# Context attention of a two-layer perceiver: nineteen score tiles in a queue, small operations moved off VectorE, keys from 96-row tiles, the last group turned in two parts

## The chip, the core and the metric

The kernel runs on one core of one Trainium2 chip. The metric is the device time of one execution in microseconds (us), as the median of several runs. The core has a matrix engine (TensorE, PE, with its weight loads shown apart as PEld), a vector engine (VectorE, DVE), a scalar engine (ScalarE, ACT), a general engine (GpSimd, POOL) and an engine that here only issues transfers (SyncE, SP). Each runs its own instructions in order; semaphores tie them together.

## The reference, cut to what matters

The whole kernel computes two layers on x (4 x 256 tokens of 256 features) with a context of 4 x 4096 vectors of 192 features. The part that the change touches is the context attention of layer 1:

```
h   = layernorm(x)                         # 4 batches x 256 tokens
q   = h @ Wq                               # 4 heads of 32
k   = ctx @ Wk                             # 4096 keys of 192 -> 4 x 32
s   = q @ k.T / sqrt(32) + mask            # per head 256 x 4096
w   = softmax over the 32 largest of each row, 0 elsewhere
c_t = mean over the 4 heads of w, @ ctx    # 256 x 192
```

The values are the context vectors themselves. c_t then steers a modulation of x, and a recurrence, a feed-forward block, self attention and a second feed-forward block follow.

## The kernel before

Layer 0 ends at about 1600 us. Then comes `l1_context` (L1073) in which 32 units of work are done: batch b (4), half of the tokens tt (2), head h (4), with 128 tokens each. Four units (the heads of one half) are a group. What one unit does:

- `scores(u)` (L1162 mask, L1165 scores, L1174 copy): 128 x 4096 scores in two steps. Each has four matmuls that add the mask and four of 32 rows that add q.k, into two PSUM tiles of 128 x 1024 from a pool of two; ACT copies each to an `sc` tile (eight of them: two units).
- `best` (L1186): 32 Max8 of DVE take the 8 largest of each 128 scores, 256 candidates in all.
- `chosen` (L1194 to L1203): four rounds of Max8 on the candidates, with a MatchReplace8 between the rounds, give the 32 largest in order (`top`). After the first round DVE makes `neg`, minus the largest (L1197). ACT computes exp(score + neg) into four tiles e of 128 x 1024 (L1201) and exp(top + neg) into `e32` (L1203).
- `weighted` (L1210 to L1216): DVE multiplies each e tile with (score >= the 32nd largest); it sums e32 (L1212), takes the reciprocal (L1213) and multiplies it by 0.25 and by a keep flag of the token (L1214). POOL multiplies the identity by that number into `diag` (L1216).
- `gathered` (L1229 to L1251) works per group, in four chunks of 1024 context positions. For each chunk 64 matmuls turn the weights: each e block of 128 x 128 is multiplied by its head's diag, and the four heads add up in PSUM (`ps_w`). Two ACT copies (L1237, `wT`) and then 16 matmuls with N = 193 (L1243) add the chunk to `ps_c`; the context tile's last column is 1, so that the weights' sum comes out too, which a later check reads. At the end ACT copies `ps_c` (L1249) and DVE takes the check (L1251).

The order is written by hand in the loop at the end of `l1_context`, and a scheduler then orders each engine's instructions by it. In the loop unit u is chosen and weighted, while unit u+1 has its Max8 and unit u+2 its scores. A group's gathering (`late`) begins at the end of its own last unit and goes on beside the next group's units: in each of them the context matmuls of one chunk, then the turning of the next one. `weights(u)` gives unit u of a group the four e tiles that hold chunk u of the preceding group, one of each head: so its exps wait for that chunk to be turned.

Beside it the keys of the next batch are computed in eight steps: `keys(b)` in `l1_context_keys` (L1032), one step in most of the units 0 to 5 of a batch, two in units 1 and 3. A step is two fp32 matmuls of 512 columns each over 128 and 64 of the 192 features (L1059, L1060) into the single PSUM tile "mm", an ACT copy to `ks` (L1062, two buffers) and four transfers that lay the heads' rows of ks into `kt` (L1064), which the scores read. The context comes in transposed, 768 KB for two steps, into two buffers (`context_keys`, L243). The single tile "mm" also serves the token transposes in unit 3 of a batch (`tokens`, L1117) and the queries in unit 6 (`queries`, L1130). `load_ctx` (L1146) loads a batch's context for the gathering into four tiles, each after a POOL memset of its last column; it is called in unit 3 of the next batch, when the gathering of the batch before is through. The keys of batch 0 are emitted ahead of the layer-0 feed-forward block and run beside its start, from 1490 us.

After the stage a flag is computed from the check and read from memory by all engines (`l1_context_again`, which holds a general version of the stage under an If); nothing of the next stage starts before that.

Of the kernel before, what the change touches and what calls it, by code (L numbers as in the profile page):

```python
# [11 lines left out]
F32 = mybir.dt.float32  # L12
# [219 lines left out]
def mask_rows(c, pool, mu):  # L232
# [10 lines left out]
def context_keys(c, pool, b, c4, queue=None):  # L243


    t = pool.tile([P, 1536], F32, tag="ctxT", name="ctxT")
    (queue or c.nc.sync).dma_start(t, c.a["ctxT"][b, c4])
    return t


def load_kk(c, pool, name, queue=None):
# [780 lines left out]
def l1_context_keys(c, es):  # L1032

    nc, tc = c.nc, c.tc
    w = Ctx()
    one = es.enter_context(tc.tile_pool(name="x1_kt", bufs=1))
    two = es.enter_context(tc.tile_pool(name="x1_ks", bufs=2))
    w.psum = es.enter_context(tc.tile_pool(name="x1_ps", bufs=1, space=PSUM))
    w.wk = load_kk(c, one, "x1_wku")
    w.wq = load_k(c, one, "x1_wq4")  # L1040
    w.keep = load(c, one, "x1_keep", [P, NB], dt=U8)
    w.kts = [one.tile([P, 4, G // 4], F32, tag=f"kt{i}", name=f"kt{i}") for i in range(2)]

    w.mask = one.tile([P, G // 4], BF16, tag="mask", name="mask")
    nc.vector.memset(w.mask, 0.0)
    w.pick = one.tile([P, B, P], BF16, tag="pick", name="pick")
    for b in range(B):
        nc.sync.dma_start(w.mask[b:P:32, :], c.mrowb[b].rearrange("(j k) -> j k", j=4))
        nc.vector.tensor_copy(w.pick[:, b, :], c.cols[:, 5 + b : 6 + b].to_broadcast([P, P]))

    def keys(b):

        kt = w.kts[b % 2]
        for c4 in range(4):
            ctxT = context_keys(c, two, b, c4)
            for j in range(2):
                hs = slice(64 * j, 64 * j + 64)
                ps = w.psum.tile([P, 512], F32, tag="mm", name="ps_k")
                nc.tensor.matmul(ps, w.wk[:, 0, :], ctxT[:, j * 512 : (j + 1) * 512], start=True, stop=False)  # L1059
                nc.tensor.matmul(ps, w.wk[hs, 1, :], ctxT[hs, 1024:1536], start=False, stop=True)  # L1060
                ks = two.tile([P, 512], F32, tag="ks", name="ks")
                nc.scalar.copy(ks, ps)  # L1062
                for h in range(4):
                    nc.sync.dma_start(  # L1064
                        kt[32 * c4 : 32 * c4 + 32, h, j * 512 : (j + 1) * 512], ks[32 * h : 32 * h + 32, :]
                    )
                yield

    w.keys = keys
    return w  # L1070


def l1_context(c, w, beside):  # L1073
# [13 lines left out]
    with ExitStack() as es:  # L1087
# [9 lines left out]

        keep = one.tile([P, NB], F32, tag="keep", name="keep")
        nc.vector.tensor_copy(keep, w.keep)
        off = one.tile([P, NB], F32, tag="off", name="off")  # L1100

        tiles = [ews.tile([P, 2, 512], F32, tag=f"e{i}", name=f"e{i}") for i in range(16)]

        def weights(u):
            h, odd = u % 4, u // 4 % 2
            return [tiles[4 * c4 + h if odd else 4 * h + c4] for c4 in range(4)]

        def tokens(b):

# [78 lines left out]
        def chosen(u):  # L1188

            top = two.tile([P, 32], F32, tag="top", name="top")  # L1190
            flat = cands.pop(u).rearrange("p n k -> p (n k)")
            for r in range(4):
                t8 = top[:, 8 * r : 8 * r + 8]
                nc.vector.max(t8, flat)  # L1194
                if r == 0:
                    neg = two.tile([P, 1], F32, tag="neg", name="neg")
                    nc.vector.tensor_scalar(neg, top[:, 0:1], -1.0, None, ALU.mult)  # L1197
                if r < 3:
                    nc.vector.match_replace(flat, t8, flat, TAKEN)
            for t, src in zip(weights(u), sc[u]):  # L1200
                nc.scalar.activation(t, src, AF.Exp, bias=neg)  # L1201
            e32 = two.tile([P, 32], F32, tag="e32", name="e32")
            nc.scalar.activation(e32, top, AF.Exp, bias=neg)  # L1203
            return top, e32

        def weighted(u, top, e32):

            b, tt, h = units[u]
            for t, src in zip(weights(u), sc.pop(u)):
                nc.vector.scalar_tensor_tensor(t, src, top[:, 31:32], t, ALU.is_ge, ALU.mult)  # L1210
            r = two.tile([P, 1], F32, tag="r", name="r")
            nc.vector.tensor_reduce(r, e32, AX.X, ALU.add)  # L1212
            nc.vector.reciprocal(r, r)  # L1213
            nc.vector.tensor_scalar(r, r, 0.25, keep[:, 2 * b + tt : 2 * b + tt + 1], ALU.mult, ALU.mult)  # L1214
            diag = two.tile([P, P], F32, tag=f"diag{h}", name=f"diag{h}")
            nc.gpsimd.tensor_scalar(diag, c.ident, r, None, ALU.mult)  # L1216
            return weights(u), diag

        def gathered(b, tt, es):

            ps_c = acc.tile([P, 512], F32, tag="acc", name="ps_c")
            n = 0
            for c4 in range(4):
                wTs = []
                for half in range(2):
                    ps = pst.tile([P, 512], F32, tag="pt", name="ps_w")
                    for i in range(4):
                        for h, (e, diag) in enumerate(es):
                            nc.tensor.matmul(  # L1229
                                ps[:, i * P : (i + 1) * P],  # L1230
                                e[c4][:, half, i * P : (i + 1) * P],
                                diag,
                                start=(h == 0),
                                stop=(h == 3),
                            )
                    wT = two.tile([P, 512], F32, tag="wT", name="wT")
                    nc.scalar.copy(wT, ps)  # L1237
                    wTs.append(wT)
                yield
                for half, wT in enumerate(wTs):  # L1240
                    for i in range(4):
                        t, j = c4 % 2 * 2 + half, c4 // 2 * 4 + i
                        nc.tensor.matmul(  # L1243
                            ps_c[:, : DC + 1], wT[:, i * P : (i + 1) * P], cxs[b][t][:, j, :], start=(n == 0), stop=(n == 31)
                        )
                        n += 1
                yield
            o = two.tile([P, DC], F32, tag="o", name="o")
            nc.scalar.copy(o, ps_c[:, :DC])  # L1249
            i = 2 * b + tt  # L1250
            nc.vector.tensor_tensor(off[:, i : i + 1], ps_c[:, DC : DC + 1], keep[:, i : i + 1], ALU.subtract)  # L1251
            nc.sync.dma_start(c.cn[:, i, :], o)
# [793 lines left out]
def _arrays(i):  # L2046
# [11 lines left out]
    for m in range(P):  # L2058
# [13 lines left out]
    ctxT = i["ctx_768"].transpose(0, 2, 1).reshape(B, DC, 4, 2, 512)  # L2072
    ctxT = np.concatenate(
        [ctxT[:, 0:P].transpose(0, 2, 1, 3, 4).reshape(B, 4, P, 1024), ctxT[:, P:].transpose(0, 2, 3, 1, 4).reshape(B, 4, P, 512)], 3
    )
    return {
        "x": i["x"],
        "ctx": i["ctx_768"],
        "ctxT": ctxT,
        "ctx6": i["ctx_768"].reshape(B, 4, 4, 256, 6, 32).transpose(0, 1, 2, 5, 4, 3).reshape(B, 4, P, 6, 256),  # L2080
        "gmask": i["mask_BxS2_bf1"].view(np.uint8),
        "cols": cols,
# [78 lines left out]
```

## Time and profile before

| | us |
|---|---|
| median of three runs (lowest, highest) | 2597.29 (2596.54, 2598.22) |
| profiled execution, its own time | 2590.52 |
| its span, first to last instruction | 2588.7 |
| mean granted TensorE clock | 0.93 |
| PE, DVE, ACT, POOL busy | 2395.8, 1658.9, 1064.9, 145.3 |
| the L1 context stage | about 1600 to 2180 |
| in it, one batch of 8 units (units 8 to 16, 16 to 24) | 143.3, 143.4 |

The profile is of one execution on the slowest core. Its busy shares are means over all stages, so a stage is read by asking the trace for its own window. A wait is listed as "engine, operation, line <- the engine, operation and line that released it". Matmul ends are modelled, so that a busy PE isn't PE at its peak. An operation's mean hides what lies beside it: the POOL operation of L1216 has a mean of 1417 ns in this stage, and single ones take from 604 to 2683 ns.

### The profile page before, as it was taken

What the parts mean: (1) busy time and instruction counts of PE and PEld (TensorE: products, weight loads), DVE (VectorE), ACT (ScalarE), POOL (GpSimd) and SP (SyncE); (2) the same over time, 40 slices, a digit from 0 to 9 for tenths busy, and PEclk for the clock granted to TensorE, in tenths of its full rate; (3) what the DMA queues carried; (4) which work ended last, traced back from release to release, by engine and by line L of the source; (5) the groups of instructions that cost most, each with busy time, mean ns of one, the idle gap of its engine ahead of it and who ended that gap; (6) DMA issues with size and microseconds to landing.
All of it is one profiled execution on the core that took longest, in us unless ns stands there. A gap on an engine that the chain in (4) does not pass through costs nothing. (4 is left out here: it accounts for less than half of the span.)

```text
span 2588.7 us, 54603 instructions
## 1 busy us (share of the span) xinstructions
PE 2395.8 (93%) x22673; PEld 1476.0 (57%) x22673; DVE 1658.9 (64%) x4043; ACT 1064.9 (41%) x1861; POOL 145.3 (6%) x176
## 2 busy tenths in 40 slices
PE   6999999999999999999899899989899988984896
PEld 4655555555555555555555544467676777453554
DVE  6666666666666666678644414988788892725544
ACT  1355554555455554556122112655555651010221
POOL 3000000000000000000000000010011010512000
PEclk7999999999999999999899989799999998996876
DMA  8321213121222213100100021203112004000110
GB/s 208 91 59 56 67 48 78 44 76 48 67 56 60 67 48 78 31 8 2 38 5 1 31 86 57 62 27 92 46 51 59 27 27 144 13 0 17 34 25 9
DMA packets 63374, 132.28 MB, mean 51 GB/s; under 512 B 11744, under 2 KB 38560, under 8 KB 62672
## 3 DMA queue, kind: packets, MB, share of 16 engines
q1 hardware_dynamic: 61616, 124.65, 17.1%
q8 instruction: 181, 2.97, 0.5%
q10 hardware_dynamic: 992, 3.02, 0.4%
q0 software_dynamic: 512, 1.05, 0.2%
q14 instruction: 73, 0.60, 0.1%
HBM read 98.17 MB, written 5.34 MB: 40 GB/s over the span
## 5 line engine op out<-in xcount | busy, mean ns | idle before, releaser
L512 DVE TENSOR_REDUCE mx<-ps_a 128x1 f32<-128x512 f32 x1024 | 659.3, 685 | 222.6 <-PE ps_a L497 218.9
L508 ACT ACTIVATE e<-ps_s 128x512 f32<-128x512 f32 x1024 | 555.7, 595 | 418.1 <-PE ps_a L497 397.8
L497 PE MATMUL ps_a<-kt,qa 32*128 32x512 f32 x2048 | 659.7, 649 | 10.9 <-DVE mx L512 7.7
L483 PE MATMUL ps_s<-qb,kt 32*128 32x256 f32 x4096 | 593.1, 402 | 0.0
L483 PEld LDWEIGHTS ps_s<-qb,kt 32*128 32x128 f32 x4096 | 350.6, 184 | 197.3 <-issue 106.4
L425 PE MATMUL o_ps<-e,v 128*32 128x256 f32 x4096 | 327.6, 391 | 0.0
L1229 PEld LDWEIGHTS ps_w<-diag,e 128*128 128x128 f32 x2048 | 242.8, 200 | 24.0 <-issue 21.7
L497 PEld LDWEIGHTS ps_a<-kt,qa 32*128 32x128 f32 x2048 | 231.8, 185 | 38.8 <-DVE mx L512 17.3
L1229 PE MATMUL ps_w<-diag,e 128*128 128x128 f32 x2048 | 248.5, 284 | 1.5 <-POOL diag L1216 1.5
L425 PEld LDWEIGHTS o_ps<-e,v 128*32 128x32 f32 x4096 | 81.0, 108 | 246.5 <-issue 235.0
L1186 DVE MAX8 cand<-sc 128x8 f32<-128x128 f32 x1024 | 212.1, 275 | 12.5 <-ACT sc L1174 12.4
L1210 DVE SCALAR_TENSOR_TENSOR e<-sc,top,e 128x1024 f32<-128x1024 f32 x128 | 159.2, 1278 | 32.7 <-ACT e L1201 32.7
L1201 ACT ACTIVATE e<-sc,neg 128x1024 f32<-128x1024 f32 x128 | 143.1, 1147 | 34.0 <-PE ps_w L1229 32.4
L1174 ACT COPY sc<-ps_s 128x1024 f32<-128x1024 f32 x128 | 126.4, 1007 | 48.0 <-PE ps_s L1165 46.3
L329 PE MATMUL ps_k<-ctxT,x_wk 32*128 32x256 f32 x1536 | 104.2, 400 | 12.4 <-DMA ctxT<-in_ctx 12.4
L351 PEld LDWEIGHTS ps_v<-x_wv,ctxT 32*128 32x128 f32 x3072 | 97.4, 190 | 15.4 <-DVE mx L512 9.4
L351 PE MATMUL ps_v<-x_wv,ctxT 32*128 32x128 f32 x3072 | 104.6, 279 | 0.7
L1243 PEld LDWEIGHTS ps_c<-cx,wT 128*128 128x128 f32 x512 | 88.6, 200 | 27.8 <-ACT wT L1237 10.6
L329 PEld LDWEIGHTS ps_k<-ctxT,x_wk 32*128 32x128 f32 x1536 | 89.1, 195 | 26.8 <-issue 18.1
L1243 PE MATMUL ps_c<-cx,wT 128*128 128x193 f32 x512 | 100.4, 349 | 2.0 <-ACT wT L1237 2.0
L824 POOL TENSOR_TENSOR x<-x,f_bo 128x256 f32<-128x256 f32 x8 | 5.8, 725 | 1538.0 <-DVE x L823 1510.8
L1165 PE MATMUL ps_s<-kt,q 32*128 32x512 f32 x512 | 87.8, 658 | 0.0
(401 smaller groups left out, 2548.3 us busy)
## 6 DMA issues: line engine op xcount, KB each, us to landing
ctxT<-in_ctx SPq DMA_DIRECT2D x62, 768.0 KB
kt<-ks SPq DMA_DIRECT2D x352, 64.0 KB
ctxT<-in_ctxT SPq DMA_DIRECT2D x16, 768.0 KB
cx<-in_ctx SPq DMA_DIRECT2D x16, 768.0 KB
x_w<-in_x_w SPq DMA_DIRECT2D x2, 1024.0 KB
qk<-rot SPq DMA_DIRECT2D x8, 256.0 KB
a_qk<-qk SPq DMA_DIRECT2D x16, 128.0 KB
ctxT<-in_ctx ACTq DMA_DIRECT2D x2, 768.0 KB
```

The lines of the kernel that those rows point to most:

```text
L329: nc.tensor.matmul(ps[:, :256], w.wk[hs, gp, k, :], ctxT[hs, k, :], start=(k == 0), stop=(k == 5))
L351: nc.tensor.matmul(ps[:, ks], ctxT[hs, k, ks], w.wv[hs, gp, k, :], start=(k == 0), stop=(k == 5))
L425: nc.tensor.matmul(o_pss[u][32 * h : 32 * h + 32, :S], vs[g // 2][:, c0 : c0 + 32], ew[h][:, n % 2, :], start=(n == 0), stop=(n == GT - 1),)
L483: nc.tensor.matmul(ps[:, k * S : (k + 1) * S], kts[u % 4 // 2][hs, u % 2, ks], qbs[u][hs, :], start=True, stop=True,)
L497: nc.tensor.matmul(ps, qas[u][hs, tt * P : (tt + 1) * P], kts[u % 4 // 2][hs, u % 2, ch * 512 : (ch + 1) * 512], start=True, stop=True,)
L508: nc.scalar.activation(e, ps.rearrange("p (k n) -> p k n", k=2), AF.Exp)
L512: nc.vector.tensor_reduce(mxs[u][:, tt, h, ch : ch + 1], ps, AX.X, ALU.max)
L1186: nc.vector.max(cands[u][:, n, :], sc[u][c4][:, i // 4, (i % 4) * P : (i % 4 + 1) * P])
L1201: nc.scalar.activation(t, src, AF.Exp, bias=neg)
L1210: nc.vector.scalar_tensor_tensor(t, src, top[:, 31:32], t, ALU.is_ge, ALU.mult)
L1229: nc.tensor.matmul(ps[:, i * P : (i + 1) * P], e[c4][:, half, i * P : (i + 1) * P], diag, start=(h == 0), stop=(h == 3),)
L1243: nc.tensor.matmul(ps_c[:, : DC + 1], wT[:, i * P : (i + 1) * P], cxs[b][t][:, j, :], start=(n == 0), stop=(n == 31))
```

## The change

There are four edits, all in the L1 context stage and its keys.

1. Nineteen e tiles in place of sixteen, given out in a queue that is computed ahead (`places`): a unit takes the four tiles at the queue's head, and the tiles of a chunk of the preceding group are put at its end. The first three tiles of a unit are thus spares, or were freed a chunk earlier; the fourth comes from the chunk just turned.
2. `neg` is computed by POOL; e32's sum is an output of ACT's exp (`accum_out`); the factor 0.25 and the keep flag are one table `quarter`, multiplied in by POOL's diag instruction. DVE keeps the reciprocal.
3. Keys from two tiles of 96 features: the context comes in another layout (`ctx96`), 384 KB for each step, and both the context tile and `ks` have one buffer.
4. The last group is gathered in two parts, heads 0 and 1, then heads 2 and 3, both into the same `ps_c`; the gathering of the group before it is pulled ahead in the units 29 and 30, and the first part's first two chunks are emitted in unit 30. The context matmuls of the last group are done for each part.

```diff
-    two = es.enter_context(tc.tile_pool(name="x1_ks", bufs=2))
-    w.wk = load_kk(c, one, "x1_wku")
+    w.wk = one.tile([96, 2, P], F32, tag="x1_wku", name="x1_wku")
+    nc.sync.dma_start(w.wk, c.a["x1_wku"].rearrange("(k p) n -> p k n", p=96))
...
         for c4 in range(4):
-            ctxT = context_keys(c, two, b, c4)
             for j in range(2):
-                hs = slice(64 * j, 64 * j + 64)
+                ctx = one.tile([96, 2, 512], F32, tag="ctx", name="ctx")
+                nc.sync.dma_start(ctx, c.a["ctx96"][b, 2 * c4 + j])
                 ps = w.psum.tile([P, 512], F32, tag="mm", name="ps_k")
-                nc.tensor.matmul(ps, w.wk[:, 0, :], ctxT[:, j * 512 : (j + 1) * 512], start=True, stop=False)
-                nc.tensor.matmul(ps, w.wk[hs, 1, :], ctxT[hs, 1024:1536], start=False, stop=True)
-                ks = two.tile([P, 512], F32, tag="ks", name="ks")
+                for k in range(2):
+                    nc.tensor.matmul(ps, w.wk[:, k, :], ctx[:, k, :], start=(k == 0), stop=(k == 1))
+                ks = one.tile([P, 512], F32, tag="ks", name="ks")
...
+        quarter = one.tile([P, NB], F32, tag="quarter", name="quarter")
+        nc.vector.tensor_scalar(quarter, keep, 0.25, None, ALU.mult)
...
-        tiles = [ews.tile([P, 2, 512], F32, tag=f"e{i}", name=f"e{i}") for i in range(16)]
+        tiles = [ews.tile([P, 2, 512], F32, tag=f"e{i}", name=f"e{i}") for i in range(19)]
+        places, free = [], list(tiles)
+        for u in range(len(units)):
+            if u > 3:
+                g, c4 = u // 4 - 1, u % 4
+                free += [places[4 * g + h][c4] for h in range(4)]
+            places.append(free[:4])
+            del free[:4]
         def weights(u):
-            h, odd = u % 4, u // 4 % 2
-            return [tiles[4 * c4 + h if odd else 4 * h + c4] for c4 in range(4)]
+            return places[u]
...
-                    nc.vector.tensor_scalar(neg, top[:, 0:1], -1.0, None, ALU.mult)
+                    nc.gpsimd.tensor_scalar(neg, top[:, 0:1], -1.0, None, ALU.mult)
...
-            nc.scalar.activation(e32, top, AF.Exp, bias=neg)
-            return top, e32
+            r = two.tile([P, 1], F32, tag="r", name="r")
+            nc.scalar.activation(e32, top, AF.Exp, bias=neg, accum_out=r)
+            return top, r
...
-            r = two.tile([P, 1], F32, tag="r", name="r")
-            nc.vector.tensor_reduce(r, e32, AX.X, ALU.add)
             nc.vector.reciprocal(r, r)
-            nc.vector.tensor_scalar(r, r, 0.25, keep[:, 2 * b + tt : 2 * b + tt + 1], ALU.mult, ALU.mult)
...
-            nc.gpsimd.tensor_scalar(diag, c.ident, r, None, ALU.mult)
+            i = 2 * b + tt
+            nc.gpsimd.tensor_scalar(diag, c.ident, r, quarter[:, i : i + 1], ALU.mult, ALU.mult)
...
-        def gathered(b, tt, es):
-            ps_c = acc.tile([P, 512], F32, tag="acc", name="ps_c")
+        def gathered(b, tt, es, ps_c, first, last):
...
-                                stop=(h == 3),
+                                stop=(h == len(es) - 1),
...
+            if not last:
+                return
...
             next(late, None)
+            if u == n - 3 or u == n - 2:
+                for _ in range(2):
+                    next(late, None)
+            if u == n - 2:
+                for _ in late:
+                    pass
+                ps_c = acc.tile([P, 512], F32, tag="acc", name="ps_c")
+                late = gathered(b, tt, group[:2], ps_c, True, False)
+                for _ in range(4):
+                    next(late, None)
...
-                late = gathered(b, tt, group)
+                if u == n - 1:
+                    late = gathered(b, tt, group[2:], ps_c, False, True)
+                else:
+                    late = gathered(b, tt, group, acc.tile([P, 512], F32, tag="acc", name="ps_c"), True, True)
```

More of the change, by code (lines that the diff above doesn't have):

```diff
@@ L240, in mask_rows @@
     nc.sync.dma_start(c.mrowb.rearrange("b (a k) -> (b a) k", k=S), mb)
[L243 to L248, printed above, removed]
 def load_kk(c, pool, name, queue=None):
@@ L1202, in chosen, with weighted @@
             e32 = two.tile([P, 32], F32, tag="e32", name="e32")
-            nc.scalar.activation(e32, top, AF.Exp, bias=neg)
-            return top, e32
-        def weighted(u, top, e32):
+            r = two.tile([P, 1], F32, tag="r", name="r")
+            nc.scalar.activation(e32, top, AF.Exp, bias=neg, accum_out=r)
+            return top, r
+        def weighted(u, top, r):
             b, tt, h = units[u]
@@ L1243, in gathered @@
                         nc.tensor.matmul(
-                            ps_c[:, : DC + 1], wT[:, i * P : (i + 1) * P], cxs[b][t][:, j, :], start=(n == 0), stop=(n == 31)
+                            ps_c[:, : DC + 1],
+                            wT[:, i * P : (i + 1) * P],
+                            cxs[b][t][:, j, :],
+                            start=(first and n == 0),
+                            stop=(last and n == 31),
                         )
@@ L2071, in _arrays @@
     causal[:, 1] = causal[:, 0].T
[L2072 to L2075, printed above, removed]
     return {
@@ L2078, in _arrays @@
         "ctx": i["ctx_768"],
-        "ctxT": ctxT,
+        "ctx96": i["ctx_768"].transpose(0, 2, 1).reshape(B, 2, 96, 8, 512).transpose(0, 3, 2, 1, 4),
         "ctx6": i["ctx_768"].reshape(B, 4, 4, 256, 6, 32).transpose(0, 1, 2, 5, 4, 3).reshape(B, 4, P, 6, 256),
```

## The prediction

> **What bounds the kernel now.** I read the page first: PE is busy 93% of the span and VectorE (DVE) 64%, but that average mixes stages. In the 40 slices of the page DVE stands at 7 to 9 tenths for eight slices on end, 26 to 33, and these are the stage that the diff touches (1600 to 2180 us). So I asked for the groups, the waits and short windows of that stage alone.
>
> The groups (line, engine, operation, shapes, count | busy us, mean ns of one | idle before it, releaser):
>
> ```profile
> L1229 PE MATMUL ps_w<-diag,e 128*128 128x128 f32 x2048 | 248.5, 284 | 1.5 <-POOL diag L1216 1.5
> L1186 DVE MAX8 cand<-sc 128x8 f32<-128x128 f32 x1024 | 212.1, 275 | 12.5 <-ACT sc L1174 12.4
> L1210 DVE SCALAR_TENSOR_TENSOR e<-sc,top,e 128x1024 f32<-128x1024 f32 x128 | 159.2, 1278 | 32.7 <-ACT e L1201 32.7
> L1243 PE MATMUL ps_c<-cx,wT 128*128 128x193 f32 x512 | 100.4, 349 | 2.0 <-ACT wT L1237 2.0
> L1194 DVE MAX8 top<-cand 128x8 f32<-128x256 f32 x128 | 54.0, 422 | 2.8
> L1199 DVE MATCH_REPLACE8 cand<-top,cand 128x256 f32<-128x256 f32 x96 | 39.2, 408 | 0.0
> L1214 DVE TENSOR_SCALAR r<-r,keep 128x1 f32<-128x1 f32 x32 | 6.7, 210 | 0.9
> L1212 DVE TENSOR_REDUCE r<-e 128x1 f32<-128x32 f32 x32 | 5.6, 174 | 3.7 <-ACT e L1203 3.7
> ```
>
> The reader sees two engines of nearly equal load. In the trace Max8 instructions start 0.195 us apart and the weighting 1.21 us apart, so one unit costs DVE 32 x 0.195 + 4 x 1.21 + 3.1 for the four rounds of the top 32 + 0.4 for the small operations = 14.6 us. PE needs 7.2 (64 turning matmuls) + 2.6 (16 context matmuls) + 2.4 (mask and scores) = 12.2, plus 2.1 for each key step: 14.3 with one key step, 16.4 with two. The shortest iterations of the stage are 14.57 us, by the starts of the turning chunks. With two key steps an iteration takes 22.2 us (1765.5 to 1787.8), with two steps and the token transposes 22.7, with queries and a key step 23.7. So each batch of 8 units loses most in three or four irregular iterations. The waits (us in total, times, longest) and the double step itself:
>
> ```profile
> DVE e L1210 <- ACT e L1201: 32.7, 26, 3.6
> ACT e L1201 <- PE ps_w L1229: 32.4, 19, 2.3
> PE ps_s L1162 <- ACT sc L1174: 24.0, 18, 1.6
> PEld ps_k L1059 <- ACT ks L1062: 12.6, 6, 2.7
> PE ps_q L1130 <- DVE q L1137: 10.0, 4, 3.0
> ```
>
> ```profile
> 1778.77 0.60 ACT L1062 COPY ks<-ps_k 128x512 f32<-128x512 f32 x1
> 1779.42 1.37 PE L1059 MATMUL ps_k<-ctxT,x_wku 128*128 128x512 f32 x2 [1.99 <-ACT ks L1062]
> 1780.72 2.07 PE L1060 MATMUL ps_k<-ctxT,x_wku 64*128 64x512 f32 x2
> 1782.87 0.58 ACT L1062 COPY ks<-ps_k 128x512 f32<-128x512 f32 x1 [3.51 <-issue]
> ```
>
> The second key step needs the one PSUM tile "mm" that the first ACT copy has to empty: PE stands 1.99 us, then ACT, in order, stands 3.51 us for the second copy, with exps behind it. The windows (length, busy us of PE, PEld, DVE, ACT, POOL, granted clock, DMA share, GB/s):
>
> ```profile
> 1765.00:1788.00 23.00, 21.01 (x122) 13.94 (x115) 20.55 (x76) 10.67 (x15) 3.42 (x4) 0.85 0.26 72
> 2120.00:2140.00 20.00, 18.04 (x146) 16.85 (x146) 18.58 (x50) 12.31 (x15) 3.21 (x2) 1.00 0.02 5
> 2140.00:2160.00 20.00, 20.00 (x167) 20.00 (x166) 1.78 (x6) 2.34 (x4) 0.00 (x0) 1.00 0.51 168
> ```
>
> Last, the end: DVE is done at about 2137, and PE turns and gathers alone until 2176, at 9.77 us a chunk. A flag is read from memory after it, and nothing of the next stage starts before 2182. So a shift of this stage's end is a shift of the whole time.
>
> **The change, part by part.** The sum is made in the profiled execution (2590.52, span 2588.7); the median of the runs, 2597.29, is 6.8 higher, and I add that at the end.
>
> *Three spare tiles.* Three of a unit's four exps no longer wait for the running turning chunk; the fourth does. The pair of waits above (32 us) is what they aim at. It is not all gain: in iterations of 14.57 DVE is never idle, and DVE's own sum is 14.6. The gain lies in the irregular iterations, counted below, and in units 24 to 28, which take 15.4 us on average instead of 14.8: -2.
>
> *Small operations off DVE.* The negation (net 0.05 us, its start to the next instruction's), the sum (L1212) and the scaling (L1214) leave: about 0.4 of 0.53 us of small work, since the reciprocal stays. Against it: before, in most units, two Max8 of the next unit are run inside the top-32 rounds and hide their dependent waits (rounds take 3.08 us so, 3.35 alone). In the changed instruction order no Max8 lies there any more. 6.24 + 4.84 + 3.4 + 0.15 = 14.65, and two short waits more make it 14.7 to 14.8. So instead of -0.4 a unit I take +0.15, on the 14 units or so that DVE bounds: +2. Bounds: -0.3 and +0.3 a unit, -5 to +5.
>
> *The negation's new place.* The exps wait for a POOL instruction. No row shows a 128x1 operation on POOL; the nearest is POOL's memset of 128x8 at 0.11 us, and with two semaphore hops I take 0.4 us; upper bound the slowest 128x128 row, 2.6. It isn't on the path: the first weighting waits for the end of the rounds 3 us later, and an exp takes 1.15, which leaves 1.8 us. What is queued on POOL in front of it are the last diag and the memsets of a new batch's context tiles (L1146), which wait for PE's last reads of the old ones: up to 12.7 us before. There the negation of units 11, 12 and their like comes after a memset that is released some 5.7 us after a turning chunk ends (scores, key step, half of the context matmuls), and is itself wanted about 5.9 to 6.5 us after it (last exp 1.15, weighting 1.2, 16 Max8 3.1, first round 0.4). Cost 0, but cover of only 2 us: a delayed PE costs its excess, six times.
> The Trainium skill, "GPSIMD Engine Reference", Specifications, says that POOL shares its SBUF interfaces with VectorE and contends when VectorE reads two SBUF inputs. The row agrees for diag: 0.60 us alone, 2.6 beside the weighting, which reads sc and e. By that rule a negation beside the rounds stays near 0.1; if it met a weighting it would be 2.6 and eat the cover.
>
> *Keys with 96 rows.* The same two fp32 matmuls of 512 columns. The rows L1059 (128 rows) and L1060 (64 rows) take 697 and 693 ns in the median of 1700 to 1790, so rows cost nothing: 0 gain on PE. The load becomes 384 KB per step instead of 768 KB per two; before, 768 KB kept the queues busy for 3.2 us. Both the context and the ks tile are now single: the second context load of a double step starts after the first step's last matmul, and the second ks copy waits until four writes have left (issue 4 x 0.58, landing 4.5 us in the median, so 6.8 us after the first copy). What saves it is the new order: the second key step lies behind the context matmuls and a mask group (2.6 + 0.6 us) or further, and its copy behind three exps and the small exp (3.8 us), which themselves wait for the next unit's rounds. So PE's 1.99 and ACT's 3.51 us go, and the half clock that followed them (0.5 from 1780.6 to 1787.0, worth 3.2 us).
> Here a rule and a row differ. "TensorE: Matmul & The Clock Gate", HAM oscillation, says that only idle gaps over about 3.4 us cost clock; by that, a gap of 2 us is worth 2 us. In this trace gaps of 1.56 and 1.99 us were followed by 3.4 and 6.4 us at clock 0.5 (another of 1.56 us was not). By the rule the double step gains 2 + 1; by the row 2 + 3.2 + some of DVE's following waits. I take the row: 22.2 becomes about 15.7, -6.5. In the token iteration the transposes wait for the same PSUM tile, now emptied by a copy late in ACT's order (a PE gap of about 3.4 us): -1. Queries: a chunk's first three turning matmuls lie between the two query halves and cover part of the 3.0 us wait: -2. One half-clock window in a single-key iteration: -0.5. Together -10 for each of the two full batches: -20 (bounds -30 and -4). Batch 0 has no turning in its first half, so PE isn't its limit: -2. The first keys, run beside the layer-0 ffn, start in a PE gap (1480 to 1489) but now go through single tiles at about 7.4 us a step: +1 (-2 to +6).
>
> *The last group in two parts.* Each chunk is turned for two heads at a time, 3.6 us instead of 7.2, but the context matmuls are done twice: 8 x (3.6 + 2.6) = 49.4 instead of 4 x 9.77 = 39.1, +10.3 of pure PE work. It would be hidden only if PE had idle time before DVE's end; the 2120 to 2140 window shows 18.04 busy of 20. From 2097 on PE has only some 5 us idle, of which the earlier start fills 2 to 3. Taken +8 (bounds -3, if PE is ahead by then, and +11).
>
> Sum: -20 - 2 - 2 + 1 + 2 + 8 = -13. Profiled 2577.5, median 2584.
>
> **The rivals.**
> *A, the forecast*: irregular iterations shrink, half of it returned at the end: 2584, between 2575 and 2591. Chance 0.42.
> *B, all of it works*: the queue of tiles also lets PE run ahead, so that heads 28 and 29 are turned before DVE ends and only 4 x 6.2 = 25 us remain after 2137 instead of 39: -14 instead of +8. 2584 - 22 = 2562. For it: in the tail DVE is idle 18 of 20 us. Against: PE's own sum in the last five units. 0.17.
> *C, nothing*: the stalls are replaced. PE's half clock comes back after the transposes and queries, each pair of iterations gains 1 or 2, and the tail takes it: -20 becomes -7, 2597. 0.19.
> *D, slower*: ACT is held at the second ks copy. If it gets there within 1 us of the first, it stands 5.8 us for the four writes, with sc, wT and exps behind it, and PE runs dry. At six double steps that is a loss of the 6.5 + 1 and 2 to 4 us more in each: 3 x 7.5 = 22, plus some 3: 2584 + 25 = 2609. It decides once landing exceeds the distance of the two copies, by my count 4 to 8 us against 6.8. 0.22.
>
> **How the numbers follow.** A measurement of this kernel tells 0.2%, 5 us, from no change: faster is below 2592.1, slower above 2602.5. A and B are faster (A's upper edge and C's lower one exchange a little): 0.60; same 0.18; slower 0.22. The range leaves a tenth at either end: into B, 2562, and into D, 2608.
>
> **What would show it.** In the profile after: the wait of L1210 on the exps falls under 15 us; no PE wait on ks above 1 us in double steps, and those iterations under 17 us; single iterations 14.6 to 14.9, not 14.2; the window after DVE's end with PE at 20 of 20 and some 45 us long. Wrong if double steps stay above 20 us (D), if ACT waits for the DMA of ks, if an exp waits for POOL by more than 2 us, or if less than 30 us lie between DVE's end and the flag (B).

## The result, and the profile after

The changed kernel takes 2561.65 us in the median of four runs (2559.07 to 2571.16) against 2596.91 (2593.97 to 2598.22): ratio 0.9872, 95% interval 0.9845 to 0.9900, some 33 us less. (Here and below, “us less” is what the ratio makes of the median before; the difference of the two medians is up to 5 us away from it.) Measured again later (e5), the ratio was 0.991 (0.9879 to 0.9941), 23 us less. The forecast was 2584, so the sign was right and the size too small; the first median lies on the low edge of the range, 2562.

The profiled execution took 2563.25, its span 2561.5, which is 27.2 less than before. The starts of the small exps (L1203 before, L1205 after), one for each unit, and the ends of a few PE groups divide that. e3 is an experiment below; up to unit 29 its code is that of the kernel before:

| stretch, us | before | e3 (before but for units 29 to 31) | after | after - before |
|---|---|---|---|---|
| start to the end of layer 0's attention output (L188) | 1478.8 | 1473.7 | 1474.0 | -4.8 |
| from there to unit 0 (first keys, layer-0 ffn) | 141.4 | 140.1 | 131.8 | -9.6 |
| units 0 to 8 | 119.8 | 121.0 | 119.9 | +0.1 |
| units 8 to 16 | 143.3 | 140.4 | 130.8 | -12.5 |
| units 16 to 24 | 143.4 | 140.2 | 132.0 | -11.4 |
| units 24 to 30 | 92.3 | 88.9 | 87.1 | -5.2 |
| unit 30 to the stage's end | 57.2 | 67.4 | 68.8 | +11.6 |
| the rest | 412.5 | 414.3 | 417.1 | +4.6 |

The first and the last row are code that the diff doesn't touch. In these runs the first row went from 1470 to 1484 and the last from 400 to 417, so single profiles are compared by stretch, not by span.

Groups of after, 1590 to 2160 us, in the columns of the prediction:

```profile
L1228 PE MATMUL ps_w<-diag,e 128*128 128x128 f32 x2048 | 241.1, 278 | 0.0
L1187 DVE MAX8 cand<-sc 128x8 f32<-128x128 f32 x1024 | 207.2, 277 | 18.3 <-ACT sc L1175 18.3
L1212 DVE SCALAR_TENSOR_TENSOR e<-sc,top,e 128x1024 f32<-128x1024 f32 x128 | 158.9, 1276 | 19.4 <-ACT e L1202 16.5
L1242 PE MATMUL ps_c<-cx,wT 128*128 128x193 f32 x576 | 105.4, 336 | 3.7 <-ACT wT L1236 3.7
L1198 POOL TENSOR_SCALAR neg<-top 128x1 f32<-128x1 f32 x32 | 6.7, 210 | 175.6 <-DVE top L1195 110.2 <-DVE off L1256 58.1 <-DVE rs_v L75 4.1
L1205 ACT ACTIVATION_READ_ACCUMULATOR e<-top,neg 128x1 f32 x32 | 6.1, 191 | 0.0
```

The last group's second pass is seen in L1242's count, 576 for 512. The sum on ACT costs a read of 0.19 us a unit and the negation on POOL 0.21. The waits (1600 to 2145) that answer to those of before:

```profile
ACT e L1202 <- POOL neg L1198: 88.5, 26, 5.6
ACT e L1202 <- PE ps_w L1228: 20.4, 11, 2.4
DVE e L1212 <- ACT e L1202: 16.5, 6, 3.5
PE ps_s L1163 <- ACT sc L1175: 14.4, 19, 2.8
PE ps_q L1131 <- DVE q L1138: 11.2, 3, 5.5
```

DVE's wait for the exps halves (32.7 to 16.5), and so nearly does PE's for the score copies (24.0 to 14.4). The longest entry, exps waiting for the negation, isn't a loss: it took the place of the small exp's wait for `top` (L1203, 104.7 us), ACT being early. POOL begins the negation within 0.17 us of the end of DVE's first round in every unit but one; in unit 12 a memset that waits for PE holds it for 1.2 us, and the unit's first weighting starts without a wait all the same. The wait for the queries' copy (11.2, and one of 5.5) stayed, and a wait for the single context buffer is new:

```profile
PE ps_k L1052 <- DMA ctx<-in_ctx: 8.6, 8, 1.8
```

A double key step of after (start us, us, engine, line, operation):

```profile
1756.80 1.98 PE L1052 MATMUL ps_k<-ctx,x_wku 96*128 96x512 f32 x4
1758.62 2.79 PE L1242 MATMUL ps_c<-cx,wT 128*128 128x193 f32 x16
1758.81 0.32 SPq L1049 DMA_DIRECT2D ctx<-in_ctx  x1
1759.27 0.62 ACT L1054 COPY ks<-ps_k 128x512 f32<-128x512 f32 x1
1761.34 0.40 PE L1163 MATMUL ps_s<-mask,pick 32*128 32x512 bf16 x4
1762.10 1.96 PE L1052 MATMUL ps_k<-ctx,x_wku 96*128 96x512 f32 x4 [0.37 <-DMA ctx<-in_ctx]
1763.99 1.14 PE L1166 MATMUL ps_s<-kt,q 32*128 32x512 f32 x8
```

The context matmuls now lie between the two key steps. They cover the ACT copy, and the second load, issued at 1758.81 after the first step, keeps PE waiting 0.37 us here, and up to 1.8 us elsewhere.

The tail, in windows (columns as in the prediction), first of the changed kernel and then of e4, which is the same without the last group's two parts:

```profile
2100.00:2120.00 20.00, 20.00 (x157) 20.00 (x156) 4.34 (x8) 4.24 (x9) 0.45 (x1) 1.00 0.51 168
2120.00:2145.00 25.00, 24.39 (x189) 24.09 (x187) 0.19 (x2) 5.00 (x9) 0.00 (x0) 1.00 0.00 1
```

```profile
2095.00:2115.00 20.00, 20.00 (x166) 20.00 (x165) 1.56 (x4) 2.34 (x4) 0.00 (x0) 1.00 0.52 164
2115.00:2132.00 17.00, 16.48 (x133) 16.18 (x131) 0.13 (x1) 2.66 (x5) 0.00 (x0) 1.00 0.00 1
```

In both PE is shown busy almost without a break; the changed kernel only has more work to do there.

### The profile page after: what moved, and what is told of

It is laid out like the page before. It is cut to its first block, busy times and chain, and to the rows that moved or that the text cites. A ratio compares the mean times of both kernels' runs of the same rounds, so it can differ in the third digit from the quotient of the medians.

```text
span 2561.5 us, 54763 instructions
## 1 busy us (share of the span) xinstructions
PE 2371.2 (93%) x22737; PEld 1470.2 (57%) x22737; DVE 1649.8 (64%) x3948; ACT 1071.5 (42%) x1901; POOL 136.3 (5%) x208
## 3 DMA queue, kind: packets, MB, share of 16 engines
q1 hardware_dynamic: 62800, 124.62, 17.7%
## 5 line engine op out<-in xcount | busy, mean ns | idle before, releaser
L1228 PEld LDWEIGHTS ps_w<-diag,e 128*128 128x128 f32 x2048 | 234.9, 194 | 24.2 <-issue 21.9
L1228 PE MATMUL ps_w<-diag,e 128*128 128x128 f32 x2048 | 241.1, 278 | 0.0
L1202 ACT ACTIVATE e<-sc,neg 128x1024 f32<-128x1024 f32 x128 | 140.7, 1143 | 119.1 <-POOL neg L1198 88.5
L1212 DVE SCALAR_TENSOR_TENSOR e<-sc,top,e 128x1024 f32<-128x1024 f32 x128 | 158.9, 1276 | 19.4 <-ACT e L1202 16.5
L321 PE MATMUL ps_k<-ctxT,x_wk 32*128 32x256 f32 x1536 | 103.7, 398 | 12.5 <-DMA ctxT<-in_ctx 11.6
L1242 PEld LDWEIGHTS ps_c<-cx,wT 128*128 128x128 f32 x576 | 97.9, 195 | 22.0 <-ACT wT L1236 9.6
L1242 PE MATMUL ps_c<-cx,wT 128*128 128x193 f32 x576 | 105.4, 336 | 3.7 <-ACT wT L1236 3.7
L1052 PE MATMUL ps_k<-ctx,x_wku 96*128 96x512 f32 x128 | 71.5, 684 | 18.5 <-DMA ctx<-in_ctx 16.0
```

Of the source, the lines that this page charges most:

```text
L321: nc.tensor.matmul(ps[:, :256], w.wk[hs, gp, k, :], ctxT[hs, k, :], start=(k == 0), stop=(k == 5))
L1228: nc.tensor.matmul(ps[:, i * P : (i + 1) * P], e[c4][:, half, i * P : (i + 1) * P], diag, start=(h == 0), stop=(h == len(es) - 1),)
L1242: nc.tensor.matmul(ps_c[:, : DC + 1], wT[:, i * P : (i + 1) * P], cxs[b][t][:, j, :], start=(first and n == 0), stop=(last and n == 31),)
```

## The experiments

Each kernel was timed against the kernel before on the same chip; its profile is one execution. An iteration is the time between the small exps of two units. A batch has two double iterations, those with two key steps; “the double iteration” is here the first of them, and the second, which has the token transposes too, is “the token iteration”. Before they take 22.0 and 20.2 us by this measure (22.2 and 22.7 in the prediction, by the starts of the turning chunks). Theory 1: the gain comes from the irregular iterations, by the place of the second key step. Theory 2: it comes from the queue of tiles. Theory 3: single buffers hold ACT.

**e1, the keys' edit alone** (edit 3 of the change, all of it):

```diff
...
-            ctxT = context_keys(c, two, b, c4)
             for j in range(2):
+                ctx = one.tile([96, 2, 512], F32, tag="ctx", name="ctx")
+                nc.sync.dma_start(ctx, c.a["ctx96"][b, 2 * c4 + j])
...
-                ks = two.tile([P, 512], F32, tag="ks", name="ks")
+                ks = one.tile([P, 512], F32, tag="ks", name="ks")
...
```

> The kernel before with the keys' edit alone (96 rows, one load a step, single buffers). Theory 1 (the gain comes from the irregular iterations: the second key step of a double iteration now lies behind the context matmuls): 17 to 24 us below before, with double iterations of 15 to 16 us in place of 22 and half-clock windows gone behind them. Theory 2 (the gain comes from the queue of tiles, which frees the exps from PE): at most 8 us below before, since the exps still wait for the running chunk. Theory 3 (single buffers hold ACT): above before.

Measured: 2579.51 against 2590.27, ratio 0.9964 (0.9948 to 0.9980), 9 us less. All of that is seen ahead of unit 0: 131.5 us in place of 140 (e3). The double iteration fell from 22 to 17.0 us, as theory 1 said, but the token iteration rose from 20 to 25.5, and the two full batches took 145.2 and 141.0: no gain. So theory 1 was half of it.

**e2, the small operations alone** (edit 2, all of it):

```diff
-                    nc.vector.tensor_scalar(neg, top[:, 0:1], -1.0, None, ALU.mult)
+                    nc.gpsimd.tensor_scalar(neg, top[:, 0:1], -1.0, None, ALU.mult)
...
-            nc.scalar.activation(e32, top, AF.Exp, bias=neg)
+            nc.scalar.activation(e32, top, AF.Exp, bias=neg, accum_out=r)
...
-            nc.gpsimd.tensor_scalar(diag, c.ident, r, None, ALU.mult)
+            nc.gpsimd.tensor_scalar(diag, c.ident, r, quarter[:, i : i + 1], ALU.mult, ALU.mult)
```

> The kernel before with the small operations' edit alone (negation on POOL, sum by ACT, factor in POOL's instruction). Theory 1: within 4 us of before, since the double iterations stay and DVE's gain of 0.4 us a unit is covered by PE's waits or lost with the interleaved Max8. Rival (DVE's own instructions bound the stage): 0.4 us for each of 32 units, 10 to 13 us below before.

Measured: 2573.67 against 2590.27, ratio 0.9956 (0.9938 to 0.9973), 11 us less. The size is the rival's, but the profile shows only part of it: units 24 to 30 take 87.4 us, where e3 and e1 without this edit take 88.9 and 88.5, which is some 0.2 us a unit and not 0.4; its batches (138.8 and 142.9, e3: 140.4 and 140.2) scatter by more than such a gain.

**e3, the last group alone** (edit 4, all of it; its last lines):

```diff
...
-                late = gathered(b, tt, group)
+                if u == n - 1:
+                    late = gathered(b, tt, group[2:], ps_c, False, True)
+                else:
+                    late = gathered(b, tt, group, acc.tile([P, 512], F32, tag="acc", name="ps_c"), True, True)
```

> The kernel before with the last group in two parts alone. By the sum of PE's work: 6 to 11 us above before (8 chunks of 6.2 us in place of 4 of 9.8, with little idle PE time to take them). Rival (the earlier start fills idle PE time): 0 to 10 us below before.

Measured: 2602.37 against 2590.27, ratio 1.0049 (1.0033 to 1.0065), 13 us more, a little over the sum; unit 30 to the end 67.4 us for 57.2.

**e4, all but the last group's parts** (edits 1, 2 and 3). Against the changed kernel:

```diff
...
-                if u == n - 1:
-                    late = gathered(b, tt, group[2:], ps_c, False, True)
-                else:
-                    late = gathered(b, tt, group, acc.tile([P, 512], F32, tag="acc", name="ps_c"), True, True)
+                late = gathered(b, tt, group)
```

> The changed kernel without the last group's two parts (it is gathered in one part, as before). By the tail of the two traces, 57.2 us before and 68.8 us after from the small exp of unit 30 to the end of the stage: 8 to 12 us below the changed kernel, so some 44 us below before. Rival (the tail is long because the gathering of the last but one group was late anyway): within 3 us of the changed kernel, about 35 us below before.

Measured: 2553.53 against 2590.27, ratio 0.9870 (0.9840 to 0.9901). Unit 30 to the end takes 56.5 us, the span is 2547.6. To compare, the changed kernel again:

> The changed kernel once more, beside others on one chip. From e4: the last group in two parts costs 10 to 13 us, so 10 to 13 us above e4's kernel as measured against before (e4: ratio 0.987), a ratio of about 0.991. Rival (the two parts cost nothing in median): 0.987, as in its first runs.

Measured: 2565.82 against 2589.65, ratio 0.9910 (0.9879 to 0.9941), the tail 68.8 us as in its first profile. The two were not run beside each other on one chip, the ratios' intervals overlap, and the changed kernel's first ratio (0.9872) is e4's; so the medians alone don't settle it. The profiles do: from unit 24 to the end of the stage the changed kernel takes 155.9 and 155.8 us and e4 144.9, some 11 more; e3, with the same edit on the kernel before, is slower clear of its interval.

**e6 and e7: the keys' edit with the queue, and with the small operations.** The queue alone was not run. Against e1:

```diff
 # e6
-        tiles = [ews.tile([P, 2, 512], F32, tag=f"e{i}", name=f"e{i}") for i in range(16)]
+        tiles = [ews.tile([P, 2, 512], F32, tag=f"e{i}", name=f"e{i}") for i in range(19)]
...
+            return places[u]
 # e7
-                    nc.vector.tensor_scalar(neg, top[:, 0:1], -1.0, None, ALU.mult)
+                    nc.gpsimd.tensor_scalar(neg, top[:, 0:1], -1.0, None, ALU.mult)
...
+            nc.scalar.activation(e32, top, AF.Exp, bias=neg, accum_out=r)
```

> Tiles' queue and keys' edit, without the small operations and the last group's parts. Theory 1a (in the token iteration the queue lets ACT pass on to the copy that the transposes wait for): token iterations 19 to 20 us in place of e1's 25.4, batches of 131 to 135 us, 25 to 33 us below before. Rival (it is the small operations that shorten the token iteration): 25 us there, batches of 140, 10 to 15 us below before.

> Small operations and keys' edit, without the queue. Theory 1a: token iterations of about 25 us stay, batches about 140 us, and the start of the stage is some 8.5 us earlier: 15 to 20 us below before. Rival: as with all three, 35 us below before.

Measured: e6 2555.92, ratio 0.9879 (0.9846 to 0.9912), 31 us less, token iterations 19.2 and 19.3, batches 130.9 and 135.0. e7 2573.24, ratio 0.9948 (0.9926 to 0.9969), 13 us less, token iterations 25.6 and 25.4, batches 139.1 and 140.6. The queue makes the token iteration short. What e1 loses there, around a turning chunk that begins at 1806.8 us (two lines ahead of it, then its end):

```profile
1803.23 0.32 ACT L1203 ACTIVATE e<-top,neg 128x32 f32<-128x32 f32 x1 [5.94 <-DVE top L1194]
1804.09 0.79 PE L1117 MATMUL ps_t<-ident,xt 128*128 128x128 f32 x4 [3.69 <-ACT ks L1062]
1807.61 8.74 PE L1229 MATMUL ps_w<-diag,e 128*128 128x128 f32 x61
1815.72 1.15 ACT L1201 ACTIVATE e<-sc,neg 128x1024 f32<-128x1024 f32 x1 [2.32 <-PE ps_w L1229]
1816.90 1.28 DVE L1210 SCALAR_TENSOR_TENSOR e<-sc,top,e 128x1024 f32<-128x1024 f32 x1 [6.66 <-ACT e L1201]
1817.24 2.19 ACT L1201 ACTIVATE e<-sc,neg 128x1024 f32<-128x1024 f32 x2
```

PE comes late to the chunk: the transposes in front of it wait 3.69 us for the second key step's ACT copy, which stands in ACT's order behind a small exp that waits 5.94 us for DVE. Then all four exps wait for the chunk's end, and DVE stands 6.66 us. The same place in e6, which differs from e1 by the queue alone:

```profile
1796.09 3.68 DVE L1216 SCALAR_TENSOR_TENSOR e<-sc,top,e 128x1024 f32<-128x1024 f32 x3
1797.18 0.66 PE L1123 MATMUL ps_t<-ident,xt 128*128 128x128 f32 x4 [0.63 <-ACT ks L1062]
1798.82 7.41 PE L1235 MATMUL ps_w<-diag,e 128*128 128x128 f32 x64
1805.60 1.15 ACT L1207 ACTIVATE e<-sc,neg 128x1024 f32<-128x1024 f32 x1 [2.32 <-PE ps_w L1235]
1806.78 1.28 DVE L1216 SCALAR_TENSOR_TENSOR e<-sc,top,e 128x1024 f32<-128x1024 f32 x1 [2.15 <-ACT e L1207]
```

Two weightings are done and the third is under way when the chunk begins; only the fourth waits, 2.15 us, and the transposes wait 0.63. So theories 1 and 2 hold together: the reorder moves the stall from the first double iteration to PE's lateness in the next, and the queue makes DVE indifferent to it. In regular units the queue by itself costs: e6 needs 15.2 us for each of units 24 to 30, e1 14.75, e4 14.73. The small operations give 0.5 us a unit back there.

**e9 and e10: which part of the keys' edit.**

```diff
 # e9: as e1, but context and ks from the pool of two
-                ctx = one.tile([96, 2, 512], F32, tag="ctx", name="ctx")
+                ctx = two.tile([96, 2, 512], F32, tag="ctx", name="ctx")
...
-                ks = one.tile([P, 512], F32, tag="ks", name="ks")
+                ks = two.tile([P, 512], F32, tag="ks", name="ks")
 # e10: the kernel before, with
-    two = es.enter_context(tc.tile_pool(name="x1_ks", bufs=2))
+    two = es.enter_context(tc.tile_pool(name="x1_ks", bufs=1))
```

> The kernel before with 96-row keys and a load of 384 KB a step, but with two buffers for context and ks. In its instruction order the second key step of a double iteration stands where it stood before. Theory 1b (e1's gain is the order that the single context buffer brings, not rows or load size): double iterations of 22 us again; the stretch from the end of layer 0's attention to the end of the layer-0 ffn 115 to 117 us as before; within 4 us of before. Rival (smaller loads and equal rows bring it): 9 us below before, that stretch 107 us.

> The kernel before with one buffer each for context and ks, rows 128 and 64 and loads of 768 KB kept. In its order the second step of the first double iteration lies behind the context matmuls, that of the token iteration does not. Theory 1b: the first double iteration 16 to 17 us in place of 22, the token one as before; some 10 us less in the three batches, less what the 768 KB loads into one buffer add: 3 to 9 us below before. Rival (single buffers cost): above before.

Measured: e9 2574.29, ratio 0.9938 (0.9915 to 0.9961), 16 us less; double iterations 21.4 and 21.7, as before; batches 139.5 and 139.8. e10 2583.07, ratio 0.9975 (0.9952 to 0.9998), 6 us less; the first double iteration 17.7, the token one 23.6 and 22.0; batches 139.0 and 137.5. So the place of the second key step comes from the single buffers, not from 96 rows. It is the context buffer: in e10's token iteration, where both steps use one load, the second step still stands in front of the context matmuls and stalls, though `ks` is single:

```profile
1820.82 1.43 PE L1059 MATMUL ps_k<-ctxT,x_wku 128*128 128x512 f32 x2 [1.99 <-ACT ks L1062]
```

Theory 3 falls as a forecast, since e10 as a whole is no slower; but its token iterations are 1 to 3 us longer than before's, and its batch 0 takes 124.5 us in place of 119.8. And without the queue the keys' edit does at least as well with double buffers (e9, 16 us less) as with single ones (e1, 9 us less, on another chip; the intervals overlap at their ends). Of e9's 16 us its profile shows some 4 ahead of unit 0 (below) and 1 to 4 in a batch; the rest stays open, and neither theory had foreseen it.

The first keys, from the end of layer 0's attention output to the end of the layer-0 ffn (L188 to the last `ps_o`): 117.0 us before, and 115.6 to 117.7 in e2, e3 and e10 to e12, with 20.5 to 23.9 us of half clock; 107.1 to 107.8 in the changed kernel and in e1, e4, e5, e6 and e8, with 6.8 us of half clock; 109.6 in e7 and 111.9 in e9, with 13.7. PE before, then after:

```profile
1476.67 2.11 PE L188 MATMUL ps_wo<-a_wo,oT 128*128 128x256 f32 x9
1489.01 1.35 PE L145 MATMUL ps_t<-ident,xn 128*128 128x128 f32 x4 [10.22 <-DVE xn L99]
1490.15 1.92 PE L1059 MATMUL ps_k<-ctxT,x_wku 128*128 128x512 f32 x2
```

```profile
1472.72 1.24 PE L188 MATMUL ps_wo<-a_wo,oT 128*128 128x256 f32 x5
1481.27 3.75 PE L1052 MATMUL ps_k<-ctx,x_wku 96*128 96x512 f32 x4 [7.31 <-DMA ctx<-in_ctx]
1484.81 2.75 PE L145 MATMUL ps_t<-ident,xn 128*128 128x128 f32 x16
```

Before, PE's first work after the gap is a transpose that waits for DVE (10.22 us). After, a key step goes first and ends the gap at 7.31. The windows (granted clock is the third number from the end) of before, then after:

```profile
1479.00:1500.00 21.00, 10.99 (x27) 4.66 (x27) 10.99 (x38) 3.83 (x6) 0.00 (x0) 0.67 0.36 121
1500.00:1520.00 20.00, 20.00 (x62) 9.75 (x62) 2.84 (x28) 4.07 (x7) 0.00 (x0) 0.74 0.37 119
```

```profile
1474.00:1495.00 21.00, 12.09 (x59) 8.11 (x60) 14.04 (x66) 3.62 (x6) 0.00 (x0) 0.84 0.32 91
1495.00:1515.00 20.00, 20.00 (x48) 7.45 (x47) 0.00 (x0) 5.93 (x10) 0.00 (x0) 1.00 0.37 109
```

PE is busy all through the second window in both, but before at clock 0.74. That is 13.7 to 17 us less at half clock, worth 7 to 8.5 us, and a gap shorter by 2.9: together a little more than the 9.6 us. The half clock comes in two pieces. The first is 13.7 us in all six profiles with a gap of 10.2 us and 6.8 in all eight with one of 7.0 to 7.8; no run changed the gap alone. The second, 6.8 or 10.2 us some 7 us later, is there in the first six and not in the changed kernel. e9, where a key step goes first too (gap 7.75), has a second piece of 6.8: further key steps lie between the transposes and the matmuls of the feed-forward block's gate (L769) instead of behind these, and PE then stands 3.23 us instead of 1.45 ahead of it. But e7, with the changed kernel's order, has a second piece without such a gap; so what brings it stays open.

**e11, e12 and e8: are double steps the loss?** One key step a unit, begun in unit 6 of the batch before, when the other `kt` is free (the keys of batch 1, in batch 0, stay as they were); in e8 and e12 also the queries in two halves, one in unit 5 and one in unit 6.

```diff
-                if u % 8 == 0:
-                    more = w.keys(b + 1)
-                for _ in range(2 if u % 8 in (1, 3) else 1):
+                if u == 0:
+                    more = w.keys(1)
+                if u % 8 == 6 and b + 2 < B:
+                    more = w.keys(b + 2)
+                for _ in range(2 if u in (1, 3) else 1):
                     next(more, None)
 # e8 and e12
-            if b + 1 < B and u % 8 == 6:
-                qs[b + 1] = queries(xT)
+            if b + 1 < B and u % 8 == 5:
+                qs[b + 1, 0] = queries(xT, 0)
+            if b + 1 < B and u % 8 == 6:
+                qs[b + 1, 1] = queries(xT, 2)
...
```

> The kernel before with one key step in each of the eight units and nothing else changed. If double steps are the loss, in the order before too: the two double iterations of each batch 14.6 to 17 us in place of 22, the step moved to unit 6 and 7 costs 2 us at most: batches about 130, 20 to 28 us below before, with none of the changed kernel's four edits. Rival (without the queue the exps hold ACT and the gain is refilled): at most 10 us.

> As e11, and the queries in two halves in two units, on the kernel before. If the queue and the small operations matter only in irregular iterations: batches of 120 to 124 us as in e8, and then e8's lead is the first keys' 8.5 us and small operations' 5 us: 45 to 55 us below before. Rival (the queue is needed for regular iterations as well): batches of 128 us or more, under 40 us below before.

> The changed kernel with the last group in one part, one key step in each of the eight units (the first batch's keys apart), and the queries in two halves, one in each of two units (two tiles q). Nothing is left out. If double steps and the query pair are what makes a batch longer than 8 x 14.7 = 118 us: batches of 119 to 123 us in place of 130.5, 18 to 25 us below e4, about 2530 us. Rival (PE with 14.3 us of work in every iteration loses its slack, and half-clock windows come back): batches of 128 us or more, at most 6 us below e4.

Measured: e11 2559.56 against 2590.52, ratio 0.9878 (0.9846 to 0.9911), 32 us less, batches 129.6 and 129.8. Double steps were the loss: moving them gives in each batch what the queue and the keys' edit gave together. e12 2550.47, ratio 0.9856 (0.9824 to 0.9887), 37 us less, batches 127.0 and 127.1: less than expected, nearer to the rival, since the token iteration still takes 18.1 and 18.6 and the next 17.0. By e1 and e6 that is the missing queue; with e12 it was not tested. e8 2519.30 against 2589.65, ratio 0.9724 (0.9687 to 0.9760), 71 us less, batches 119.8 and 121.0 against the 118 of eight regular units. It is the fastest of all, and clearly below both kernels; its token iteration takes 15.2 to 15.3. By the medians that is 34 us below e4 (on another chip), more than expected: batch 0 gains too, 110.9 us for e4's 120.3, since its iteration with the queries of batch 1 goes from 25.3 to 15.5. Waits of e8, 1700 to 1960 us:

```profile
ACT e L1209 <- POOL neg L1205: 66.8, 14, 5.6
ACT e L1209 <- PE ps_w L1236: 3.1, 4, 1.2
```

In this stretch of 260 us the exps wait 3.1 us for PE, and the list has no wait of DVE at all. DVE is busy 252.8 us of it and PE is shown busy 258.8 at full clock, with ends that are modelled: both are close to full. That units 24 to 30, without key steps, take the same 14.7 us speaks for DVE as the limit.

## Why the prediction was right or wrong

**Right in the double iteration.** Forecast 22.2 to 15.7; by the small exps 22.0 to 16.0 and 15.0 in its two batches, with the second step where the prediction put it. A full batch: forecast -10, measured -12.5 and -11.4, or -9.6 and -8.2 against e3's profile of the same code. Regular units: 14.7 as said. The negation: its first-round Max8 ended at 1764.58, the exps began at 1764.98, the 0.4 us of the estimate. Rival D fell: no wait of ACT for the kt writes is listed in the stage. (Its sum, 3 x 7.5, counts three of the six double steps that it speaks of.)

**The clock: the row was right and the rule was not.** In the profile before, from unit 8 to DVE's end, no gap of PE is longer than 2.98 us, yet there are eleven stretches of half clock, 51.2 us in all, each beginning at a gap of 1.56 to 2.98 us or within 1.4 us behind it. By the rule of the Trainium skill that the prediction set aside ("TensorE: Matmul & The Clock Gate", HAM oscillation: no idle gaps over about 3.4 us) they would have cost no clock. After, it is 17.1 us. But that is not all the double step's: e3 has 30.7 us with the order before, and e1, with the double step moved, still 34.1. (The stretch behind the double step that was shown lasts 6.8 us, from 1780.2 to 1787.0, not 6.4.)

**Not told apart: whose the -10 is.** The prediction counted it under the keys' edit, the queue's share in irregular iterations included, and gave the queue 2 us elsewhere. e1 shows that the keys' edit by itself gains nothing in a batch, since the token iteration grows from 20 to 25.5 us; with the queue (e6) the batches take 130.9 and 135.0. The working had the transposes' gap (“about 3.4 us”; e1 shows 3.69) and still took the iteration as 1 us shorter; that the queue closes the gap (0.63 in e6) and makes this come true, it did not say.

**Two of its signs.** DVE's wait for the exps was to fall under 15 us and fell to 16.5. An exp that waits for POOL by more than 2 us was to show it wrong; there are such waits, up to 5.6 us, but they are ACT's idle time: POOL itself was late by more than 1 us only once.

**The step that failed: the first keys, "+1 (-2 to +6)".** It came out at -9.6, beyond the bound, and every kernel with the whole keys' edit shows it. The prediction saw that the first step fell into PE's gap, and priced it as work moved. It did not price the clock: with the gap broken at 7.3 us instead of 10.2, and the other order behind it, two thirds of some 20 us at half clock are gone. The row that told it was in the prediction itself (half clock after a gap), used for the double step and not here.

**Mis-sized: the last group, "+8".** +11.6 in its stretch, but the cut at unit 30 adds 1.3 to that, as this unit's small exp comes earlier in the changed order (13.4 us behind unit 29's for 14.7 in e4). From unit 24 to the end the changed kernel takes 11.0 us more than e4, and e3 10.1 more than e9: the bound of 11, or the +10.3 of pure work. Nothing of the second pass was hidden, and the early start gained nothing.

**Mis-sized: the queries, "-2" a batch.** From unit 15 to 16 the interval went from 23.1 to 22.5, and from 23 to 24 from 23.1 to 25.5: -0.6 and +2.4. The wait of 10 us stayed. In its place others gave more than was forecast: from unit 8 to 16 the token iteration -0.7 and the next -0.6 (forecast -1 together), the unit after the first double step -1.5 (not forecast), and the unit that had half clock in before's profile -2.9 (forecast -0.5).

**Right sum, wrong owner: the small operations, "+2".** e2 alone gains 11 us. The loss that I put down to them, rounds without interleaved Max8, comes with the queue: in the units 24 to 30 two Max8 lie between a unit's rounds in e1, e2 and e7, and none in e4 and e6 (15.2 us a unit in e6). The small operations repay it. The two cancel in the changed kernel, so its 14.7 looked like the forecast.

**Partly chance.** Units 24 to 30, -5.2: e3, with nearly the same code there, took 88.9, so 3.4 us of it is that before's profile had half clock in every second unit; 1.3 is the cut at unit 30. The forecast's -2 for the queue is then some 0.5. Batch 0 gave nothing instead of -2.

In sum: -13 was -20 - 2 - 2 + 1 + 2 + 8; the stretches gave -23.9 (batches), -5.2, +0.1, -9.6 and +11.6, and the untouched code -4.8 and +4.6: -27.2.

## What to carry to other kernels

Where an average unit fits its engines and a few units do not, look for what is doubled up in those few and spread it: a few lines in the loop (e11) gave as much as the four edits, and with three of them kept and the queries halved (e8) the gain was twice that. Price a PE gap with the half clock that follows it, also for work that only moves into the gap. Before work is done twice to start earlier, check in a window ahead of the end that the engine has room: PE had 2 us in 20 here, and the second pass cost its full price.

## What the runs showed of the hardware

Half-clock windows came in multiples of 3.4 us in all profiles (but for the last of each, which the profile's end cuts), and their place differs between executions of the same code: units 24 to 30 of the old code took 92.3 us in one profile and 88.9 in another, and the kernel before ran from 2575 to 2599 us over three chips. One such piece in untouched code, from 1261 to 1283 us, cost the profile before 9 us: PE had 0.57 and 0.50 of the clock in two windows of 10 us there, and 0.97 and 1.00 in the profile after.
